# Attention scores in tiles of 64 rows by 32 columns: each block of 32 queries with its own keys only

## The chip, the cores and the metric

The kernel runs on one core of one Trainium2 chip. A core has TensorE (matmuls and the loads of their weights, "PE" and "PEld" in the profile), VectorE ("DVE"), ScalarE ("ACT"), GpSimd ("POOL") and SyncE ("SP", which issues most transfers). The metric is the device time of one execution in microseconds; three runs gave a median of 1027.56 us (1027.11 to 1027.65).

## The reference

The input x holds 64 sequences of 128 tokens with 512 features, in float32. One attention layer is added to it:

```
xn  = layernorm(x, g_in)
q   = (xn @ Wq) as 16 heads of 64, * 64 ** -0.5
k,v = xn @ Wkv, one head of 64 shared by all 16; a null key and a null value are put in front
sim = q @ k + bias            # 16 x 128 x 128 bias, one more for the null key
sim = causal mask, then the mask of the sequence's own tokens
out = softmax(sim) @ v, heads side by side, @ Wo
x   = x + layernorm(out, g_out)
```

A query i sees the null key and keys 0 to i alone. Everything is float32; on TensorE a float32 matmul is carried out in two passes, each a weight load and a matmul.

## The kernel before

**Work and stages.** The 64 sequences are worked in pairs. A *cycle* c handles the softmax of the pair b0, b1, the output product of the pair before (p), the layer norm of the one before that (r), and prepares queries, keys and values for later ones (m). The query projections and the output products are computed as Strassen-like sums: `q_one(c, k, h)` is product k of the query projection for half h, `leaf(c, k, stage)` splits three of them once more, and `out_one(p, k)` is product k of the output. A cycle ends with a *region* (line 1057): the scores of the next pair n0, n1, then the product of probabilities and values of b0, b1. The loop over cycles 1 to 29 calls `cycle` (line 1078); cycle 0 and the end are written out (from line 1294 and from line 1457).

**Order.** The schedule is manual: the order of calls in the source is the order of instructions on every engine, and all that an engine does waits behind what was called before it. TensorE's instructions lie in program blocks of 256; `nc.tensor.addr_align(256, offset=n)` fills up with empty instructions so that the next instruction stands on slot n of a block. It is called once per cycle, ahead of `leaf(c, 3, 0)` (line 1215), and four times in the part before the cycles.

**Layout of the scores.** The 128 queries of a sequence are 4 blocks of 32 (`Q` = 32, `NQ` = 4), the 128 keys likewise. The 16 heads are split over u (2), f (4) and r (2). The 128 rows of a score tile are 4 groups of 32, s = 2 i + u: i tells which query block, u which half of the heads. There are two tiles for a sequence: the lower one (hf = 0) holds query blocks 0 and 1 against the first 64 keys, the upper one (hf = 1) query blocks 3 (i = 0) and 2 (i = 1) against all 128 keys. So no query is multiplied with more than the keys of its tile, though block 0 has 32 keys too many in the lower one and block 2 has 32 too many in the upper one. What is too much is driven to a very negative value by the bias: `bias_add` (POOL, line 631) lays the bias with the causal mask and the mask of the sequence into the score buffer `S[b]` beforehand.

**Scores.** `heads(b, hf, to)` (line 645) makes, for each f, r and i, one matmul with a stationary operand of 64 rows (head features, half r of the partitions) by 64 columns (2 u x 32 queries), and the keys of the tile as the moving operand. That is 16 matmul calls a tile. Four such calls (2 r x 2 i) fill the four quadrants of the array. The results go to banks of PSUM: the upper tile of n0 to `ps_s`, the lower tiles of both to banks a and c of `ps_q`, the upper tile of n1 to the two banks of `ps_w`. `scores_add` (line 682) then adds a tile's banks into `S[b]` on DVE: one addition for the upper tile of n0, two for each other one. `scores_max` and `exps` (ACT) make the softmax from it; `blocks_T` transposes the probabilities on DVE, and `values` multiplies them with the values, in tiles of 32 rows by 64 columns.

**Head of a cycle.** After the region, TensorE goes on with `q_one(c, 1, 0)` (product 1 into bank a), `q_one(c, 5, 0)` (bank c), `leaf(c, 2, 0)` and `q_one(c, 6, 0)` (again bank a). Between products, ACT copies bank a out (`first_into`, line 502). ACT also has to move the values' results out of PSUM (`values_out`, line 794), and DVE the maxima of the scores. From cycle 2 on (`LEAF` = 2) `q_one(c, 7, h)` and `q_one(c, 8, h)` each add bank c into a part of the queries on DVE (lines 1008 and 1016).

Of the kernel before, what the change touches and what calls it, by code (L numbers as in the profile page):

```python
# [8 lines left out]
FP = mybir.dt.float32  # L9
# [8 lines left out]
def kernel(  # L18
# [625 lines left out]

    def heads(b, hf, to):
        g, t = divmod(b, GB)
        for f in range(NF):
            for r in range(2):
                rows = slice(r * DH, (r + 1) * DH)
                for i in range(2):  # L650
                    nc.tensor.matmul(  # L651
                        to[r][i * DH : (i + 1) * DH, f, :],
                        qT[g, f // FH, t // GH][
                            rows, f % FH, t % GH, NQ - 1 - i if hf else i
                        ],
                        kT[g][rows, 0 : NQ if hf else NQ // 2, t, :],
                        start=True,
                        stop=True,
                    )

    def scores_upper(b, pool, tags):
        if len(tags) == 1:
            ps = pool.tile([P, 2, NF, N], FP, tag=tags, name=f"ps_{b}_1")
            heads(b, 1, [ps[:, r] for r in range(2)])
            pss[b, 1] = [(slice(0, R8), ps)]
        else:
            ps = [pool.tile([P, NF, N], FP, tag=t, name=f"ps_{b}_1{r}") for r, t in enumerate(tags)]
            heads(b, 1, ps)
            pss[b, 1] = [(slice(r * NF, (r + 1) * NF), ps[r]) for r in range(2)]

    def scores_lower(bs):
        low = [
            ps_q.tile([P, 2, NF, NL], FP, tag="ac"[r], name=f"ps_{bs[0]}_0{r}")
            for r in range(2)
        ]
        for k, b in enumerate(bs):
            heads(b, 0, [low[r][:, k] for r in range(2)])
            pss[b, 0] = [(slice(r * NF, (r + 1) * NF), low[r][:, k]) for r in range(2)]

    pss = {}  # L680

    def scores_add(b, hf):
        for ks, ps in pss.pop((b, hf)):
            sv = S[b][:, ks, KEYS[hf]]
            if ks.stop - ks.start == R8:
                sv = sv.rearrange("p (r f) j -> p r f j", r=2)
            nc.vector.tensor_tensor(sv, ps, sv, ALU.add)  # L687

# [291 lines left out]
    def q_one(c, k, h):  # L980
# [12 lines left out]
        elif k == 2:  # L993
            product(g, f, 2, ps_w, "w")
            q_out(g, f, lo_t, "w", "p1")
        elif k == 5:
            product(g, f, 5, ps_q, "c")
        elif k == 6:
            product(g, f, 6, ps_q, "a", start=False)
            if c >= LEAF:  # L1000
                first_into(g, f, 1)
            else:
                keep("a", "u2")
        elif k == 7:
            product(g, f, 7, ps_q, "a", start=False)
            if c >= LEAF:
                first_into(g, HC + f, 0)
                nc.vector.tensor_tensor(
                    q_part(g, HC + f, 1), by_block("c"), q_part(g, HC + f, 0), ALU.add
                )  # L1010
            else:
                keep("a", "u3")
                q_out(g, HC + f, hi_t, "c", "u3")
        elif k == 8:
            o = q_part(g, f, 1)
# [62 lines left out]
    def cycle(c):  # L1078
# [21 lines left out]
        if pair:  # L1100
            values_out(p + 1, (0, 2))
        if fin:
# [304 lines left out]
    bias_add(2)  # L1407
    nc.tensor.addr_align(256, offset=40)
    q_one(0, 3, 0)
# [9 lines left out]
    q_one(0, 1, 1)  # L1419
    nc.tensor.addr_align(256, offset=97)  # L1420
    q_one(0, 2, 1)
# [6 lines left out]
    bias_add(3)  # L1428
    nc.tensor.addr_align(256, offset=146)
    q_one(0, 6, 1)  # L1430
# [9 lines left out]
    leaf_weights(4, 2)  # L1440
    nc.tensor.addr_align(256, offset=211)
    q_one(0, 4, 1)
# [198 lines left out]
```

## Time and profile before

| | |
|---|---|
| median of three runs | 1027.56 us |
| span of the profiled execution | 1024.9 us |
| TensorE matmuls busy | 1013.0 us, 12,104 instructions |
| TensorE weight loads busy | 900.7 us, 12,104 instructions |
| VectorE busy | 852.5 us |
| GpSimd busy | 788.2 us |
| ScalarE busy | 642.8 us |
| matmuls of the scores (line 651) | 4,096 instructions, 93.7 us |
| program blocks fetched for TensorE | 96 packets, 1.57 MB |

In a row of groups there stand the source line, the engine, the operation, what is written and read, the shape (for TensorE the tile of the array, rows * columns, then the moving operand), the count, then the busy time, the mean duration of one, and the idle time of the engine before them with what ended it. In a row of the timeline the start and the length of one or more merged instructions come first, both in us. A row of a stretch gives its start and end, its length, then for each engine the busy time and, in brackets, the number of instructions that ran in it, then the granted clock, the DMA share and GB/s. Where a row names no engine order, the order is PE, PEld, DVE, ACT, POOL. A row of the queues gives packets, MB, and the time of the packets as a share of 16 engines over the stretch. Rows of one line's instructions give count, shortest, median and longest duration, and the first and last start; `PEldq` is TensorE's instruction sequencer.

### The profile page before, as it was taken

The numbers are of one execution on the slowest core, as the hardware profiler recorded it, in microseconds if no ns is written. First come the engines' busy times: TensorE is split into PE (matmuls) and PEld (weight loads), VectorE is DVE, ScalarE is ACT, GpSimd is POOL, SyncE is SP. The second block draws the span as 40 slices with busy tenths as digits, with TensorE's granted clock in tenths as the row PEclk, the third lists the DMA queues.
The fourth block names the chain that finished last, engine by engine and source line by source line (L and its number), as shares of the span: only waits on it lengthen the run. The fifth ranks groups of instructions, "written<-read, shape, count | busy, mean of one in ns | idle before, by whom it ended". The sixth has DMA issues, their size and how long they took to land. (4 is left out here: it accounts for less than half of the span.)

```text
span 1024.9 us, 31793 instructions
## 1 busy us (share of the span) xinstructions
PE 1013.0 (99%) x12104; PEld 900.7 (88%) x12104; DVE 852.5 (83%) x2000; ACT 642.8 (63%) x2742; POOL 788.2 (77%) x710
## 2 busy tenths in 40 slices
PE   9999999999999999999999999999999999999997
PEld 8888888888888889888889888889888898888876
DVE  6776887888888888888888878788888888878798
ACT  2655776555776556775556765557765567755591
POOL 3799959688696878959689596887968789596874
PEclk9999999999999999999999999999999999999999
DMA  7542350524315152241623505253151521402203
GB/s 212 165 125 55 104 135 26 158 64 135 107 43 152 49 158 84 93 118 32 171 71 106 135 23 158 64 140 101 46 152 46 157 85 73 111 25 67 84 2 104
DMA packets 70264, 100.91 MB, mean 98 GB/s; under 512 B 27744, under 2 KB 31328, under 8 KB 68320
## 3 DMA queue, kind: packets, MB, share of 16 engines
q1 hardware_dynamic: 69008, 97.83, 33.1%
q8 instruction: 96, 1.57, 0.7%
q10 hardware_dynamic: 1104, 1.05, 0.3%
q14 instruction: 56, 0.46, 0.2%
HBM read 63.19 MB, written 33.55 MB: 94 GB/s over the span
## 5 line engine op out<-in xcount | busy, mean ns | idle before, releaser
L701 ACT ACTIVATE s<-s,nmax 128x65 f32<-128x65 f32 (+1 forms) x1024 | 382.2, 413 | 3.5 <-DVE nmax L692 3.5
L701 ACT ACTIVATION_READ_ACCUMULATOR s<-s,nmax 128x1 f32 x1024 | 242.0, 236 | 0.0
L722 POOL TENSOR_TENSOR s<-s,rinv 128x1024 f32<-128x1024 f32 (+1 forms) x128 | 189.4, 1482 | 46.4 <-DVE rinv L718 46.4
L635 POOL TENSOR_TENSOR s<-biasp,mneg 128x1552 f32<-128x1552 f32 x64 | 205.0, 3224 | 2.0 <-DMA x<-in_x_dram 2.0
L810 ACT ACTIVATE oT<-poX,nv 128x256 f32<-128x256 f32 x58 | 27.5, 474 | 219.2 <-PE poX L770 113.0
L687 DVE TENSOR_TENSOR s<-ps,s 128x256 f32<-128x256 f32 (+2 forms) x224 | 120.0, 605 | 15.7 <-PE ps L651 15.2
L556 DVE TENSOR_TENSOR qT<-pl,qT 128x128 f32<-128x128 f32 (+1 forms) x420 | 122.4, 323 | 3.3 <-PE pl L553 3.3
L860 PE MATMUL pyX<-wo,oT 128*128 128x256 f32 x512 | 121.4, 380 | 0.0
L692 DVE TENSOR_REDUCE nmax<-s 128x8 f32<-128x520 f32 (+1 forms) x128 | 116.5, 949 | 0.1
L860 PE MATMUL pyX<-wT,oT 128*128 128x256 f32 x488 | 115.7, 380 | 0.7 <-POOL oT L843 0.7
L737 DVE STREAM_TRANSPOSE sb<-s 128x1536 f32<-128x1536 f32 x64 | 113.1, 1768 | 0.6 <-POOL s L722 0.6
L860 PEld LDWEIGHTS pyX<-wo,oT 128*128 128x128 f32 x512 | 97.0, 190 | 14.3 <-issue 0.9
L917 POOL TENSOR_TENSOR rstdo<-rstdo,nhalf 128x1 f32<-128x1 f32 x64 | 35.0, 548 | 91.5 <-DVE rstdo L913 91.5
L860 PEld LDWEIGHTS pyX<-wT,oT 128*128 128x128 f32 x488 | 88.4, 191 | 10.8 <-POOL oT L843 1.1
L651 PE MATMUL ps<-kT,qT 64*64 64x128 f32 (+1 forms) x4096 | 93.7, 246 | 0.4 <-issue 0.4
L651 PEld LDWEIGHTS ps<-kT,qT 64*64 64x64 f32 x4096 | 85.5, 134 | 5.5 <-issue 2.1
L770 PE MATMUL pos<-sb,vr 32*64 32x128 f32 (+1 forms) x1792 | 81.4, 321 | 0.0
L843 POOL TENSOR_TENSOR yS<-oT 128x512 f32<-128x512 f32 x32 | 40.8, 1274 | 45.4 <-ACT oT L810 42.0
L770 PE MATMUL poY<-sb,vr 32*64 32x128 f32 x720 | 74.6, 348 | 0.0
L770 PE MATMUL poX<-sb,vr 32*64 32x128 f32 x960 | 73.5, 299 | 0.0
L503 ACT COPY qT<-pa 128x256 f32<-128x256 f32 x168 | 68.2, 406 | 1.4 <-PE pa L597 1.4
L331 DVE STREAM_TRANSPOSE xb<-x 128x512 f32<-128x512 f32 x56 | 39.4, 705 | 34.1 <-ACT x L310 34.1
(150 smaller groups left out, 2545.6 us busy)
## 6 DMA issues: line engine op xcount, KB each, us to landing
res<-in_x_dram SPq DMA_DIRECT2D x64, 256.0 KB, 2.9
out_dram<-y SPq DMA_DIRECT2D x58, 256.0 KB, 2.1
x<-in_x_dram SPq DMA_DIRECT2D x224, 64.0 KB, 2.0
xd<-xb SPq DMA_DIRECT2D x14, 1024.0 KB, 4.3
xT<-xd SPq DMA_DIRECT2D x56, 256.0 KB, 5.4
vr<-vd SPq DMA_DIRECT2D x64, 128.0 KB, 3.3
x<-in_x_dram SPq DMA_DIRECT2D x8, 256.0 KB, 4.8
vd<-vt SPq DMA_DIRECT2D x32, 64.0 KB, 6.2
```

The costliest lines, as they stand in the source:

```text
L503: nc.scalar.copy(q_part(g, c, h), by_block("a"))
L556: nc.vector.tensor_tensor(o, p, o, ALU.add)
L635: nc.gpsimd.tensor_tensor(S[b], biasp, mneg[:, t].unsqueeze(1).broadcast_to([P, R8, ROW]), ALU.add,)
L651: nc.tensor.matmul(to[r][i * DH : (i + 1) * DH, f, :], qT[g, f // FH, t // GH][rows, f % FH, t % GH, NQ - 1 - i if hf else i], kT[g][rows, ...
L687: nc.vector.tensor_tensor(sv, ps, sv, ALU.add)
L692: nc.vector.tensor_reduce(nmax[b][:, hf], S[b][:, :, WITH_NULL[hf]], AX.X, ALU.max, negate=True)
L701: nc.scalar.activation(row, row, AF.Exp, bias=nmax[b][:, hf, k : k + 1], accum_out=rsum[b][:, hf, k : k + 1],)
L722: nc.gpsimd.tensor_tensor(sv, sv, rinvs.pop((b, hf)).unsqueeze(2).broadcast_to([P, R8, sv.shape[2]]), ALU.mult,)
L737: nc.vector.transpose(sb.rearrange("p j e q -> p e j q"), S[b][:, :, 1 : ROW - 1].rearrange("p e (j k) -> p e j k", k=Q),)
L770: nc.tensor.matmul(po[s][rows, half], vr[g][quad(s), j, t, :], sb[quad(s), slots, r * NF : (r + 1) * NF, :], start=start, stop=True, skip_ ...
L843: nc.gpsimd.tensor_tensor(o, l, m, op)
L860: nc.tensor.matmul(prod[key], h[:, c, :], w[:, c, :], start=(start and c == 0), stop=(c == HC - 1), skip_group_check=not start,)
```

## The change

The scores are made of tiles of 64 rows by 32 columns, eight to the array: u is no longer part of the stationary operand's columns, and each block of 32 queries is multiplied with the keys of blocks 0 to its own alone (32, 64, 96 or 128 of them). `region` first reserves the banks of all four tiles and then hands all four to one `heads`, which interleaves them: for each i the columns already streamed are summed up (`at`), and the runs of four calls (2 r x 2 u) are issued in the order of that sum, so that both halves of the array's columns progress alike. In this program each call of `heads` for a region makes 128 matmul calls instead of 64.

`scores_add` makes two additions of each one: all 128 rows for the keys that both query blocks have, and the 64 rows of the later block for the 32 keys beyond.

In the head of a cycle, from cycle 2 on, `q_one(c, 1, 0)` is called one `values_out` earlier (its copy on ACT then stands ahead of the pair's last `values_out` on banks X and Y), the two first `exps` are called behind `q_one(c, 6, 0)`, the addition that belonged to `q_one(c, 7, h)` is made by `q_one(c, 8, h)`, which stands behind `out_one(p, 2)` in the first half and ahead of `leaf(c, 4, 1)` in the second. All alignments move by 27 slots.

```diff
+    def heads(parts):
+        runs = []
+        for i in range(2):
+            at = 0
+            for b, hf, to in parts:
+                block = NQ - 1 - i if hf else i
+                for f in range(NF):
+                    runs.append((at, i, b, block, f, to))
+                    at += block + 1
+        for _, i, b, block, f, to in sorted(runs, key=lambda run: run[:2]):
+            g, t = divmod(b, GB)
+            for r in range(2):
+                rows = slice(r * DH, (r + 1) * DH)
+                for u in range(2):
+                    s = 2 * i + u
+                    nc.tensor.matmul(
+                        to[r][quad(s), f, 0 : (block + 1) * Q],
+                        qT[g, f // FH, t // GH][rows, f % FH, t % GH, block, u],
+                        kT[g][rows, 0 : block + 1, t, :],
+                        start=True,
+                        stop=True,
+                        tile_position=(r * DH, s * Q),
+                    )
...
     def scores_add(b, hf):
+        first = KEYS[hf].start
+        ends = (Q, 2 * Q) if hf == 0 else (3 * Q, 4 * Q)
         for ks, ps in pss.pop((b, hf)):
-            sv = S[b][:, ks, KEYS[hf]]
-            if ks.stop - ks.start == R8:
-                sv = sv.rearrange("p (r f) j -> p r f j", r=2)
-            nc.vector.tensor_tensor(sv, ps, sv, ALU.add)
+            for rows, lo, hi in (
+                (slice(0, P), 0, ends[0]),
+                (slice((1 - hf) * DH, (2 - hf) * DH), ends[0], ends[1]),
+            ):
+                sv = S[b][rows, ks, first + lo : first + hi]
+                if ks.stop - ks.start == R8:
+                    pv = ps[rows, :, :, lo:hi]
+                    sv = sv.rearrange("p (r f) j -> p r f j", r=2)
+                else:
+                    pv = ps[rows, :, lo:hi]
+                nc.vector.tensor_tensor(sv, pv, sv, ALU.add)
...
     def region(c):
-            scores_upper(n0, ps_s, "s")
-            scores_lower((n0, n1))
-            scores_upper(n1, ps_w, "ww")
+            up0 = score_banks(n0, ps_s, "s")
+            low = lower_banks((n0, n1))
+            up1 = score_banks(n1, ps_w, "ww")
+            heads([(n0, 1, up0), (n0, 0, low[0]), (n1, 0, low[1]), (n1, 1, up1)])
...
     def cycle(c):
         if pair:
-            values_out(p + 1, (0, 2))
+            values_out(p + 1, (0,))
+        early = c < LEAF or p < 0
+        if not early:
+            q_one(c, 1, 0)
+        if pair:
+            values_out(p + 1, (2,))
...
-        q_one(c, 1, 0)
+        if early:
+            q_one(c, 1, 0)
...
-        if soft:
-            exps(b0, 0, 0, 2)
         q_one(c, 6, 0)
         if soft:
-            exps(b0, 0, 2, 8)
+            exps(b0, 0)
...
+        out_one(p, 2)
         if c >= LEAF:
             q_one(c, 8, 0)
-        out_one(p, 2)
...
-            nc.tensor.addr_align(256, offset={1: 120, B // 2 - 3: 76}.get(c, 94))
+            nc.tensor.addr_align(256, offset={1: 147, B // 2 - 3: 103}.get(c, 121))
...
         if c >= LEAF:
+            q_one(c, 8, 1)
             leaf(c, 4, 1)
-            q_one(c, 8, 1)
```

`score_banks` and `lower_banks` are the parts of the former `scores_upper` and `scores_lower` that reserve banks; at the end of the kernel these two still exist and call `heads` for one or two tiles.

More of the change, by code (lines that the diff above doesn't have):

```diff
@@ L643, with score_banks, lower_banks @@
     WITH_NULL = slice(0, 1 + NL), slice(1 + NL, ROW)
[L645 to L661, printed above, removed]
+    pss = {}
+    def score_banks(b, pool, tags):
         if len(tags) == 1:
             ps = pool.tile([P, 2, NF, N], FP, tag=tags, name=f"ps_{b}_1")
-            heads(b, 1, [ps[:, r] for r in range(2)])
             pss[b, 1] = [(slice(0, R8), ps)]
[L666 to L671, printed above, removed]
+            return [ps[:, r] for r in range(2)]
+        ps = [pool.tile([P, NF, N], FP, tag=t, name=f"ps_{b}_1{r}") for r, t in enumerate(tags)]
+        pss[b, 1] = [(slice(r * NF, (r + 1) * NF), ps[r]) for r in range(2)]
+        return ps
+    def lower_banks(bs):
         low = [
@@ L676, in scores_lower, with scores_upper @@
         for k, b in enumerate(bs):
[L677 removed]
             pss[b, 0] = [(slice(r * NF, (r + 1) * NF), low[r][:, k]) for r in range(2)]
[L680 removed]
+        return [[low[r][:, k] for r in range(2)] for k in range(len(bs))]
+    def heads(parts):
[21 more added lines that the diff above has]
+                    )
+    def scores_upper(b, pool, tags):
+        heads([(b, 1, score_banks(b, pool, tags))])
+    def scores_lower(bs):
+        low = lower_banks(bs)
+        heads([(b, 0, low[k]) for k, b in enumerate(bs)])
     def scores_add(b, hf):
+        first = KEYS[hf].start
+        ends = (Q, 2 * Q) if hf == 0 else (3 * Q, 4 * Q)
         for ks, ps in pss.pop((b, hf)):
[L684 to L687 removed]
+            for rows, lo, hi in (
[9 more added lines that the diff above has]
+                nc.vector.tensor_tensor(sv, pv, sv, ALU.add)
     def scores_max(b, hf):
```

14 lines of the change are left out of this document (7 added, 7 removed).

## The prediction

> **What bounds the kernel now.** I read the page first, then the groups by form, then stretches of one cycle, and last the instruction queue of TensorE.
>
> ```profile
> span 1024.9 us, 31793 instructions
> PE 1013.0 (99%) x12104; PEld 900.7 (88%) x12104; DVE 852.5 (83%) x2000; ACT 642.8 (63%) x2742; POOL 788.2 (77%) x710
> PEclk9999999999999999999999999999999999999999
> q8 instruction: 96, 1.57, 0.7%
> ```
>
> TensorE has no idle time to give (1013.0 of 1024.9 us), so whatever lengthens its stream lengthens the kernel. The last row is the transfer of its program: 96 packets in 1.57 MB are 16 KB each, and 24,208 matmuls and weight loads over 96 are 252, so a packet is a block of some 256 instructions.
>
> The scores, by form (matmuls, weight loads, the DVE additions that follow), and the two stages of one cycle, scores (499.07 to 501.91) and values (to 504.36):
>
> ```profile
> L651 PEld LDWEIGHTS ps<-kT,qT 64*64 64x64 f32 x4096 | 85.5, 134 | 5.5 <-issue 2.1
> L651 PE MATMUL ps<-kT,qT 64*64 64x128 f32 x2048 | 69.2, 273 | 0.0
> L651 PE MATMUL ps<-kT,qT 64*64 64x64 f32 x2048 | 35.9, 218 | 0.4 <-issue 0.4
> L687 DVE TENSOR_TENSOR s<-ps,s 128x256 f32<-128x256 f32 x128 | 45.2, 413 | 0.0
> L687 DVE TENSOR_TENSOR s<-ps,s 128x1024 f32<-128x1024 f32 x32 | 39.2, 1224 | 15.7 <-PE ps L651 15.2
> ...
> core 0: us, PE busy (x), PEclk, DMA share, GB/s
> 499.07:501.91 2.84, 2.84 (x130) 1.00 0.51 119
> 501.91:504.36 2.45, 2.45 (x116) 1.00 0.88 224
> ```
>
> A region multiplies four score blocks (upper and lower keys of two sequences): 64 calls, each two passes, each a weight load and a matmul: 128 matmuls, 256 instructions in 2.84 us.
>
> **Part 1: the smaller tiles.** *Columns.* A column group streams, per sequence and pass, 4 heads x (128 + 64) = 768 columns today and 4 x (128 + 32) or 4 x (96 + 64) = 640 afterwards, a sixth less. Of the 2.84 us about 0.2 are the change of tile shape, so the stream shrinks from 2.64 to 2.20 us: 0.44 us saved per region, if nothing but the array counts.
>
> *Instructions.* The same work becomes 128 calls, so 512 instructions instead of 256. Can they be supplied? The weight loads of the lower blocks; the stretch before the values (matmuls, then loads); and the marks that the instruction sequencer leaves when it passes into the values (source line 770) and out of them (597):
>
> ```profile
> core 0: us, PEld busy (x), PEclk, DMA share, GB/s
> ...
> 499.98:500.92 0.94, 0.94 (x68) 1.00 0.59 174
> ...
> 501.30:501.91 0.61, 0.61 (x29) 0.44 (x17) 0.61 (x3) 0.00 (x0) 0.00 (x0) 1.00 0.85 121
> ...
> L770 PEldq EVENT_SEMAPHORE  x2: 51/51/51, 501.2 to 501.3; - x2
> ...
> L597 PEldq EVENT_SEMAPHORE  x2: 51/51/51, 503.7 to 504.0; - x2
> ```
>
> In the lower blocks 64 loads and 64 matmuls, 128 instructions, go in 0.93 us: 7.3 ns each, but from a filled queue. Between the marks at 501.3 and 503.7 the sequencer passes the 224 instructions of the values: 10.7 ns each, one block change included. Between these two ends I take 8.3 ns, the value at which weight loads for idle tiles arrive when the queue is dry:
>
> ```profile
> 502.60 0.13 PEld L770 LDWEIGHTS pos<-sb,vr 32*64 32x64 f32 x1
> 502.62 0.13 PEld L770 LDWEIGHTS poX<-sb,vr 32*64 32x64 f32 x1
> 502.62 0.13 PEld L770 LDWEIGHTS pos<-sb,vr 32*64 32x64 f32 x1
> ```
>
> The two loads of pos lie about 17 ns apart, and a load and its matmul are two instructions. At that rate 512 instructions need 4.25 us; the queue holds some 40 at the start (an estimate: when the sequencer marks the values at 501.3, the 29 + 17 score instructions of the second row are still running or to come), which takes off 0.33. So the region would be bound by its instructions at 3.9 us, not by the array at 2.2: 1.3 us more per region (0.8 at 7.3 ns, 2.4 at 10.7).
>
> [...]
>
> *Blocks.* The 256 added instructions are one more program block per region, three where two lie now. The queue's packets around a region, in this order: from 529.8 to 533.7; from 498.8 to 505.5; from 505.5 to 509.4; then one packet in 1.8 us from 498.85, and one in 1.8 us from 809.55:
>
> ```profile
> q8 instruction: 2, 0.03, 4.0%
> ...
> q8 instruction: 1, 0.02, 1.3%
> ...
> q8 instruction: 2, 0.03, 4.2%
> ...
> q8 instruction: 1, 0.02, 4.7%
> ...
> q8 instruction: 1, 0.02, 6.0%
> ```
>
> A packet starts at each end of the first and third windows: 3.8 and 3.8 us apart. Between these, in the cycle that sends the transposed tokens out and back (1 MB each way, DMA share 0.88 in the values), one is 6.7 us after the other. The last two rows are transfers of 16 x 1.8 x 4.7% = 1.35 us and 1.73 us; and only after the long one did the values stop:
>
> ```profile
> 809.70:812.54 2.84, 2.84 (x129) 2.67 (x128) 2.78 (x7) 0.00 (x0) 1.75 (x1) 1.00 0.75 183
> 812.54:815.27 2.73, 2.73 (x116) 2.21 (x112) 2.73 (x6) 0.00 (x0) 0.00 (x0) 1.00 0.89 222
> ...
> 812.73 0.27 PE L770 MATMUL poY<-sb,vr 32*64 32x128 f32 x2
> 812.89 0.32 PE L770 MATMUL pos<-sb,vr 32*64 32x128 f32 x2
> ```
>
> 2.73 us instead of 2.45, with a hole up to 812.89. I read this so: entering a block asks for the next one, which is usable 3.5 us later (the 3.8 us less some room; more under heavy transfers), and there is room for no more than these two. Today blocks change about every 3.7 us here, so it just fits. Afterwards the region starts on a block (the aligned point moves from slot 94 to 121, and 133 instructions of the cycle's code lie between it and the region, which so begins at slot 254 instead of 227): the middle of the region is reached after (258 - 40) x 8.3 = 1.8 us, and only then is the block of the values asked for. It is usable at 1.8 + 3.5 = 5.3 us, and in the cycles with the token transfers 6.7 - 3.8 = 2.9 us later, at 8.2. The values start at 2.84 today. So the price, which contains the 1.3 us above, is 2.5 us in a quiet region and 5.4 in a busy one. Ends: no wait for blocks, 1.3; a busy region with the block still later, 7.
>
> [...]
>
> **Part 2: additions in two.** 7 instructions per region become 14, over the same elements per lane. From 413 ns at 256 and 1224 at 1024 elements, one costs 1.06 ns per element and 0.14 us: 224 x 0.14 = 31 us more on DVE at most, 884 of 1025. They run beside the values and the next products; the longer region covers them. Without that cover: 1 us a cycle. They also must wait for the first upper block, after 36 of 128 calls (16 of 64 today): about the same share.
>
> **Part 3: the head.** What TensorE loses there, by the timeline:
>
> ```profile
> 504.36 1.13 PE L597 MATMUL pa<-xT,wq 128*128 128x256 f32 x4
> 505.33 1.03 PE L597 MATMUL pc<-xS,wS 128*128 128x256 f32 x4
> 506.44 1.13 PE L597 MATMUL pa<-xS,wS 128*128 128x256 f32 x4
> ...
> 506.00 0.39 ACT L503 COPY qT<-pa 128x256 f32<-128x256 f32 x1
> 506.25 1.61 ACT L810 ACTIVATE oT<-pos,nv 128x256 f32<-128x256 f32 x4
> ```
>
> Product 6 waits 0.1 us for ACT's copy of bank a. That copy now goes ahead of one values_out, and the next one ahead of two exponentials, so the 0.1 us goes: 28 x 0.1 = 3 us gained; late next is nothing that the trace shows. TensorE's own order is not changed by these moves. On DVE the additions from bank c come after out_part of product 2 (second half: after tokens_T and out_part, and ahead of leaf 4's two): one addition of 0.41 us in front of two others, and no matmul waits there now; nothing. No DMA and no POOL step moves. The program's alignment by 27 slots costs nothing but the block position above.
>
> **The sum.** 31 regions, 30 with values; the token transfers lie in 14. 16 x 2.5 + 14 x 5.4 = 116; first region 1.3 and the end's three score calls about 1.5; head -3. Together +115 on the profiled execution (span 1024.9; the median of the runs is 2.7 above it, which I leave outside): 1027.6 + 115 = about 1142 us.
>
> **Rivals.** (1) *Supply alone.* Blocks are there in time and only the 8.3 ns count: 31 x 1.3 + 1 - 3 = +38, 1066 us (1049 at 7.3 ns, 1099 at 10.7). For it: the values from 501.91 pass in 2.45 us without such a hole. Against: the hole at 812.89. (2) *The array decides, the change is faster.* If instructions come at under 4.3 ns (2.2 us over 512), each region gains 0.44: 31 x 0.44 + 3 = 17, 1011 us. [...] For it: bursts of loads a few ns apart. Against: the dry stretches and the marks above; from 5.6 ns on ((512 - 40) x 5.6 = 2.64 us) nothing of it is left. (3) *Nothing changes*, gain and supply meet by chance: about 1028.
>
> [...]
>
> **How the numbers follow.** Blocks and supply (forecast) 0.60, its own range 1102 (all regions quiet) to 1170 (busy ones at 7); supply alone 0.26; faster 0.12; no change 0.02. A measurement tells some 0.2% from no change. Leaving out the faster case and the ends of the others gives 1050 to 1178. Faster 0.12, same 0.02, slower 0.86.
>
> **What would show it.** The scores' matmuls 8192, PEld count 16,200. Right: the stage from first score to first value matmul lasts 5.3 us and more, the values still about 2.5 us, with holes in TensorE before the values that are longer where DMA share is high, PE share well under 99%, and q8 at 128 packets. Supply alone would show stages of 4.1 us, all alike. Wrong altogether if that stage lasts under 2.84 us: then the rate of 8.3 ns belonged to the values' own tiles.

## The result, and the profile after

The changed kernel takes 1181.74 us (median of four runs, 1178.7 to 1186.24) against 1027.49 us before: 1.1506 times the time, 95% interval 1.1489 to 1.1523. It is 154 us slower; 115 were forecast, and the range ended at 1178. The profiled execution has a span of 1176.9 us, 152.0 more than before.

From the page of the changed kernel (busy time and instructions of each engine, the granted clock in 40 slices, the queue of TensorE's program, two groups), and behind it, from the page before, the first of these two groups:

```profile
span 1176.9 us, 40240 instructions
PE 1062.2 (90%) x16200; PEld 946.5 (80%) x16200; DVE 891.9 (76%) x2224; ACT 644.3 (55%) x2742; POOL 786.0 (67%) x710
...
PEclk9889989899998999989899898998989999899999
...
q8 instruction: 128, 2.10, 0.7%
...
L795 PE MATMUL poX<-sb,vr 32*64 32x128 f32 x960 | 108.8, 383 | 90.0 <-issue 90.0
...
L681 PEld LDWEIGHTS ps<-kT,qT 64*32 64x32 f32 x8192 | 99.3, 105 | 14.3 <-issue 10.7
```

```profile
L770 PE MATMUL poX<-sb,vr 32*64 32x128 f32 x960 | 73.5, 299 | 0.0
```

TensorE now idles for 10% of the span, and 90 us of that stand ahead of one group: the first bank of the values (line 795, which was 770 and had no idle time). "issue" says that no semaphore the profile shows released it. The packets of the program are 128, as many as predicted. New is the clock row: TensorE no longer has full speed everywhere.

Three stretches of a region, first in a cycle with the transfers of the tokens (14), then in a quiet one, without them (15): the scores up to the first value instruction, the hole, the values behind it (start and end, length, busy time and instructions by engine, granted clock, DMA share, GB/s):

```profile
574.45:577.67 3.22, 3.22 (x257) 3.07 (x256) 3.12 (x9) 0.00 (x0) 1.96 (x1) 1.00 0.69 165
577.67:583.22 5.55, 0.07 (x4) 0.13 (x1) 5.37 (x15) 0.00 (x0) 0.55 (x1) 0.76 0.93 199
583.22:587.28 4.06, 4.06 (x112) 3.85 (x111) 2.25 (x4) 0.00 (x0) 0.00 (x0) 0.50 0.20 58
613.24:616.46 3.22, 3.22 (x257) 3.07 (x256) 2.41 (x8) 0.00 (x0) 3.22 (x3) 1.00 0.03 5
616.46:618.40 1.94, 0.32 (x4) 0.13 (x2) 1.83 (x7) 0.00 (x0) 1.94 (x3) 1.00 0.00 0
618.40:620.66 2.26, 2.26 (x110) 2.18 (x111) 2.19 (x8) 0.00 (x0) 0.57 (x1) 1.00 0.04 7
```

The scores take 3.22 us in both, 0.38 more than before. Then TensorE stands still, 1.94 us in the quiet cycle and 5.55 us where the DMA engines are 93% busy. Behind the long hole the values run at a granted clock of 0.50, called half clock below, and take 4.06 us in place of 2.26. (These stretches end where the last value matmul starts; counted so, the values took 2.15 us before.)

The hole itself, from the timeline of the weight loads (PEld) and of the matmuls (PE):

```profile
577.67 0.13 PEld L795 LDWEIGHTS poX<-sb,vr 32*64 32x64 f32 x1
583.22 0.29 PEld L795 LDWEIGHTS poX<-sb,vr 32*64 32x64 f32 x3 [5.42 <-issue]
...
583.22 0.48 PE L795 MATMUL poX<-sb,vr 32*64 32x128 f32 x2 [5.48 <-issue]
```

One weight load of the values is carried out, and the matmul that belongs to it comes 5.5 us later. The region begins on slot 254; two instructions fill that block, 512 instructions of the scores fill two more but for two slots, and the wait and the first load of the values take these (in cycle 15, where no such wait stands, the first load and its matmul). The hole is exactly where a block ends. It isn't a wait of the values for their operands: that wait was over when the load ran.

The next block arrives ahead of the hole's end. The queue of TensorE's program over 1.4 us, from 580.50 in cycle 14 and from 615.68 in cycle 15:

```profile
q8 instruction: 1, 0.02, 6.0%
...
q8 instruction: 1, 0.02, 5.9%
```

The two packets take 1.35 and 1.31 us. They start 6.07 and 2.46 us into the region, and the values go on 1.35 and 1.39 us after the packet's end. In all of the cycles 0 to 28 the hole ends 1.3 to 1.6 us after the end of such a packet, and the packet takes 0.9 to 1.5 us, with and without the transfers of the tokens. What differs is its start: 2.3 to 3.0 us into the region without them, 4.4 to 6.6 us with them. So the transfers don't stretch the packet, they delay its start; by what way is not shown.

Put together over the cycles (mean differences from before, each taken in the two traces from the first score of one region to that of the next):

| | cycles | first value | values go on | values behind the hole | rest of the cycle | cycle | sum |
|---|---|---|---|---|---|---|---|
| with token transfers (0, 2 to 26) | 14 | +0.38 | +5.43 | +1.79 | +0.14 | +7.36 | 103.1 |
| without (1 to 27, but 5) | 13 | +0.38 | +2.11 | +0.08 | -0.20 | +1.99 | 25.9 |
| 5 and 28 | 2 | +0.38 | +2.44 | +1.41 | +0.10 | +3.95 | 7.9 |
| the first (c = -1) | 1 | | | | | +9.3 | 9.3 |
| 29 and the end | 1 | | | | | +6.2 | 6.2 |

"Values go on" holds "first value" in it. With -0.4 us ahead of the first region the sum is 152.0, the whole difference of the spans.

### The profile page after: what moved, and what is told of

Same layout as the page of the kernel before. It is cut to its first block, busy times and chain, and to the rows that moved or that the text cites. A ratio compares the mean times of both kernels' runs of the same rounds, so it can differ in the third digit from the quotient of the medians.

```text
span 1176.9 us, 40240 instructions
## 1 busy us (share of the span) xinstructions
PE 1062.2 (90%) x16200; PEld 946.5 (80%) x16200; DVE 891.9 (76%) x2224; ACT 644.3 (55%) x2742; POOL 786.0 (67%) x710
## 5 line engine op out<-in xcount | busy, mean ns | idle before, releaser
L726 ACT ACTIVATION_READ_ACCUMULATOR s<-s,nmax 128x1 f32 x1024 | 235.2, 230 | 0.0
L795 PE MATMUL poX<-sb,vr 32*64 32x128 f32 x960 | 108.8, 383 | 90.0 <-issue 90.0
L712 DVE TENSOR_TENSOR s<-ps,s 128x128 f32<-128x128 f32 (+2 forms) x448 | 160.8, 382 | 28.3 <-PE ps L681 23.1
L795 PEld LDWEIGHTS poX<-sb,vr 32*64 32x64 f32 x960 | 86.2, 174 | 96.2 <-issue 91.9
L942 POOL TENSOR_TENSOR rstdo<-rstdo,nhalf 128x1 f32<-128x1 f32 x64 | 35.1, 549 | 128.5 <-DVE rstdo L938 128.4
L681 PE MATMUL ps<-kT,qT 64*32 64x32 f32 (+3 forms) x8192 | 107.5, 238 | 8.5 <-issue 8.5
L681 PEld LDWEIGHTS ps<-kT,qT 64*32 64x32 f32 x8192 | 99.3, 105 | 14.3 <-issue 10.7
L795 PE MATMUL pos<-sb,vr 32*64 32x128 f32 (+1 forms) x1792 | 109.6, 404 | 0.0
L795 PE MATMUL poY<-sb,vr 32*64 32x128 f32 x720 | 103.0, 447 | 2.7 <-issue 2.7
L743 DVE RECIPROCAL rinv<-rsum 128x8 f32<-128x8 f32 x128 | 23.7, 186 | 91.8 <-ACT s L726 91.7
```

The source lines that it names most:

```text
L681: nc.tensor.matmul(to[r][quad(s), f, 0 : (block + 1) * Q], qT[g, f // FH, t // GH][rows, f % FH, t % GH, block, u], kT[g][rows, 0 : block ...
L712: nc.vector.tensor_tensor(sv, pv, sv, ALU.add)
L726: nc.scalar.activation(row, row, AF.Exp, bias=nmax[b][:, hf, k : k + 1], accum_out=rsum[b][:, hf, k : k + 1],)
L795: nc.tensor.matmul(po[s][rows, half], vr[g][quad(s), j, t, :], sb[quad(s), slots, r * NF : (r + 1) * NF, :], start=start, stop=True, skip_ ...
L942: nc.gpsimd.tensor_tensor(yn[b][1], yn[b][1], nhalf, ALU.pow)
```

## The experiments

The forecast's theory is that a program block of 256 instructions is usable some 3.5 us after the block ahead of it was entered (its estimate, from packets 3.8 us apart), later under transfers. Its rivals: the values wait for something that the change makes late; small tiles or many instructions cost by themselves. Each run is compared with the kernel before on the same chip; the ratio's 95% interval is in brackets.

**Own keys without small tiles.** The new scores, additions and head, but tiles of 64 rows by 64 columns, so 256 instructions a region; once with all alignments 10 slots later (region on slot 8), once as in the kernel after (slot 254).

```diff
-                for u in range(2):
-                    s = 2 * i + u
-                    nc.tensor.matmul(to[r][quad(s), f, 0 : (block + 1) * Q],
-                        qT[...][rows, f % FH, t % GH, block, u], kT[g][rows, 0 : block + 1, t, :],
-                        ..., tile_position=(r * DH, s * Q))
+                nc.tensor.matmul(to[r][i * DH : (i + 1) * DH, f, 0 : (block + 1) * Q],
+                    qT[...][rows, f % FH, t % GH, block], kT[g][rows, 0 : block + 1, t, :], ...)
...
-    nc.tensor.addr_align(256, offset={1: 147, B // 2 - 3: 103}.get(c, 121))
+    nc.tensor.addr_align(256, offset={1: 157, B // 2 - 3: 113}.get(c, 131))   # slot 8 alone
```

> The kernel after with tiles of 64 rows by 64 columns (so 256 instead of 512 instructions in a region) that are multiplied with their own keys only, and all alignments 10 slots later, so that a region begins on slot 8 of a program block. Theory of the program blocks (a block is usable some 3.5 us after the one ahead of it was entered): the block ends lie 248 instructions into the region and 24 instructions behind its end; the block after next is asked for at about 1.8 us and usable at 5.2 to 5.3, when TensorE is not yet through with the 24 instructions of the head. So no hole: the first score to the first value matmul takes 2.4 us, the values 2.15, granted clock 1.00 throughout, 0.44 us less per region and 3 to 5 us for the head: 1009 to 1013 us. Rival (the values wait for a semaphore that the new order or the split additions make late): holes of 1.6 us and more stay ahead of the values, 1080 us and over. Rival (weight loads for 64 columns do not fit in 32 streamed columns): scores stay at 2.8 us, about 1023 us.

> As the run with slot 8, but with the alignments of the kernel after, so that the region begins on slot 254 and the values on a block. Theory of the program blocks: the second block of the region is entered some 0.4 us ahead of the region, the third is usable some 3.1 us into it, the values would begin at 2.4: a hole of 0.5 to 0.8 us at the first value matmul in quiet regions, longer by up to 3 us in regions with the token transfers: 1015 to 1050 us, at least 5 us slower than with slot 8. Rivals that do not know of blocks: the same time as with slot 8 within 2 us.

Measured: 1070.34 us on slot 8 (1.0418 [1.0402, 1.0433]) and 1051.47 us on slot 254 (1.024 [1.0223, 1.0257]). With 256 instructions there is no hole between scores and values at all, so what the values wait for in the kernel after is neither the new order nor the additions. Nearly everything else in these two expectations failed. The stages of a quiet cycle on slot 254 (scores, values), then from its timeline a matmul of product 1 of the second half:

```profile
415.80:418.63 2.83, 2.83 (x129) 2.65 (x128) 2.09 (x7) 0.00 (x0) 2.83 (x2) 1.00 0.00 0
418.63:420.78 2.15, 2.15 (x115) 2.04 (x112) 2.02 (x8) 0.00 (x0) 2.15 (x3) 1.00 0.03 8
```

```profile
428.88 0.70 PE L597 MATMUL pa<-xT,wq 128*128 128x256 f32 x2 [0.40 <-ACT qT L503]
```

The scores take 2.83 us with 640 columns streamed per column group, sequences and passes as in the prediction, where they took 2.84 with 768. So in tiles of 64 columns the number of streamed columns did not set the time of the scores, and the 0.44 us were not to be had. The last rival of the first expectation, that the loads of 64 weight columns take this long, named 2.8 us and agrees; no run tests it by itself. And the quiet cycles are 31.55 us, 0.46 longer than before, from a wait for ACT's copy of bank a. On slot 254 no hole is seen in quiet cycles, where 0.5 to 0.8 us were expected: the second block's packet starts 2.28 us ahead of the region, not 0.4. By an estimate TensorE's instruction sequencer is then at least some 25 instructions ahead: in the trace of the kernel after, 23 to 25 matmuls and weight loads start in the 2.28 us ahead of a region (cycles 9, 11, 14 and 15). In its cycles with transfers the next block, which begins 514 instructions behind the region's start, is late in the output product of the next head (by 1.66 us in cycle 12); from cycle 2 on they take 31.6 to 32.6 us. On slot 8 the block behind the values comes late in the cycles with transfers, in the products of the next head (timeline, cycle 12):

```profile
463.78 0.27 PE L553 MATMUL pl<-xT,wq 128*128 128x128 f32 x1
465.77 0.27 PE L553 MATMUL pl<-xT,wq 128*128 128x128 f32 x1 [1.71 <-issue]
```

Its packet started at 462.78 us. These cycles take 32.2 to 35.3 us. So the theory of blocks also says why slot 8 is the worse one, but that was seen afterwards.

**Additions alone.** The kernel before with `scores_add` of the kernel after.

> The kernel before with the additions in two alone (scores, head and alignments as before). Theory, after the run with 64-column tiles, where every quiet cycle had one wait of 0.66 us at the first product of the second half: the seven more additions (7 x 0.14 us) push DVE's maxima and with them ACT's exponentials and its copy of bank a behind the point at which TensorE wants it, and only the longer regions of the kernel after cover this. Then 0.4 to 0.7 us in 29 cycles: 1040 to 1048 us. Rival, as the prediction has it (hidden beside other work): 1027.5 us.

Measured: 1055.01 us (1.0273 [1.0257, 1.0289]). From its timeline:

```profile
424.70 0.81 PE L870 MATMUL pyX<-wo,oT 128*128 128x256 f32 x3
426.07 1.13 PE L597 MATMUL pa<-xS,wq 128*128 128x256 f32 x4 [0.56 <-ACT qT L503]
```

A cycle takes 32.01 us in place of 31.09: TensorE waits for ACT's copy of bank a. On ACT that copy stands behind exponentials, and these wait for DVE's maxima, which stand behind the additions (that this is the way the delay takes is read from the order of the calls). More than expected: 28 us. In the kernel after the rest of a quiet cycle is 0.20 us shorter than before, so there the longer region does hide all of it.

**Head alone.** The kernel before with the cycle's head (and product 8's addition) of the kernel after.

> The kernel before with the new head of the cycle alone (scores, additions and alignments as before). In the trace after the change, the part of a quiet cycle from the last value matmul to the next region lasts 25.91 us against 26.10 before. Theory (the head frees TensorE of a wait on ACT's copy of bank a): 0.1 to 0.2 us in 28 cycles, 3 to 5 us faster, 1022.5 to 1024.5 us. Rival (the shorter rest comes from work that the longer region hides): no difference, 1027.5 us. If the head costs something, over 1028 us.

Measured: 1031.0 us (1.0031 [1.0013, 1.0048]), ten runs from 1024.54 to 1033.4. A quiet cycle is 30.90 us against 31.09, as expected; but some of the cycles with transfers lose more than all that. Cycle 26 (scores, hole, what is left of the values):

```profile
873.32:876.16 2.84, 2.84 (x130) 2.67 (x129) 2.78 (x7) 0.00 (x0) 1.95 (x1) 1.00 0.88 220
876.16:879.03 2.87, 0.46 (x18) 0.23 (x15) 2.84 (x7) 0.00 (x0) 0.00 (x0) 1.00 1.05 212
879.03:882.11 3.08, 3.08 (x99) 2.87 (x98) 3.04 (x7) 0.00 (x0) 0.55 (x1) 0.64 0.56 123
```

A block comes late with 256 instructions too, and the clock falls (0.64 over the third stretch). Here the packet started 2.86 us into the region; before, 0.14 us ahead of it.

**The block end moved.** The kernel after with 128 added to the offset of every alignment (249 in place of 121 in most cycles), so that the region begins on slot 126.

> The kernel after, all alignments 128 slots later: the region begins on slot 126. Theory of the program blocks: there are two holes in a quiet region, one behind instruction 386 of the scores (from 2.3 to about 4.0 us) and one in the middle of the values, behind instruction 642 (about 1.4 us), and none between the scores and the values; a quiet cycle takes 34 to 34.8 us in place of 33.1, one with transfers 39 to 42; 1205 to 1260 us. Rival (the hole belongs to the values, by a semaphore or a buffer): it stays at their first instruction, and the time stays within 1165 to 1195 us.

Measured: 1208.69 us (1.177 [1.1749, 1.1792]). One quiet cycle (9): scores, hole, scores up to the values and their first half, hole, second half:

```profile
418.66:420.85 2.19, 2.19 (x194) 2.19 (x193) 1.41 (x5) 0.00 (x0) 2.19 (x2) 1.00 0.03 7
420.85:422.69 1.84, 0.25 (x22) 0.06 (x9) 0.36 (x2) 0.00 (x0) 1.84 (x2) 1.00 0.00 0
422.69:424.95 2.26, 2.26 (x127) 2.05 (x128) 1.86 (x7) 0.00 (x0) 1.63 (x2) 1.00 0.03 7
424.95:426.25 1.30, 0.24 (x11) 0.00 (x0) 1.26 (x5) 0.00 (x0) 0.00 (x0) 1.00 0.00 0
426.25:427.19 0.94, 0.94 (x47) 0.85 (x47) 0.94 (x3) 0.00 (x0) 0.00 (x0) 1.00 0.00 0
```

The hole has left the first value instruction and stands inside the scores, behind 194 + 193 instructions (386 were predicted), at 2.2 us; a second one is in the middle of the values. The work and its waits are the same: the holes move with the block ends. The quiet cycles take 34.2 to 35.1 us, the time lies at the lower end of what was expected. Not all of the loss against the changed kernel is in the regions: 12 of the 30 us between the profiled executions lie in the first cycle (51.10 us in place of 39.15), where the alignments put in 128 more empty instructions.

**The reads of the tokens moved.** The kernel after with the four reads (1 MB) behind the next cycle's fetch of the values in SP's queue.

```diff
         if first and toks:
             tokens_out(m // GB)
...
-        if first and toks:
-            tokens_in(m // GB)
...
             values_fetch(fetch)
+        if not first and LEAF < c and m - 2 < B:
+            tokens_in((m - 2) // GB)
```

> The kernel after, with the reads of the transposed tokens (1 MB in four transfers) moved in SP's queue from ahead of a region to behind the next cycle's fetch of the values, so that they run after the region. Theory (the transfers hold up the program block by 2 to 4 us, and the longer hole also lets the granted clock fall to half): the regions with token transfers become like the others, hole of 1.5 to 2.2 us in place of 3.9 to 5.9, values 2.26 us in place of 4.06, cycles of 33 us in place of 38: 13 x 5 = 65 to 75 us faster than the kernel after, 1105 to 1120 us. Rival (the holes of these regions have another cause, such as work of the even cycles on DVE or POOL): no change, 1180 us.

Measured: 1131.22 us (1.1024 [1.0998, 1.105]): 50 us less than the changed kernel, not 65 to 75. Cycle 14 (first value, hole, values):

```profile
552.89:556.42 3.53, 3.41 (x257) 3.15 (x256) 3.13 (x9) 0.00 (x0) 1.94 (x1) 1.00 0.22 36
556.42:558.68 2.26, 0.08 (x3) 0.13 (x1) 2.15 (x7) 0.00 (x0) 0.00 (x0) 1.00 0.36 75
558.68:562.41 3.73, 3.73 (x111) 3.53 (x111) 3.66 (x10) 0.00 (x0) 0.55 (x1) 0.57 0.58 159
```

The hole is 2.26 us in place of 5.55. But the scores are 0.3 us longer (a block is late inside them too), and the clock still fell in eight of these cycles.

**The writes left out as well.** The same, and from the fourth group on no write of the transposed tokens.

```diff
     def tokens_out(g):
+        if g > 2:
+            xbs.pop(g)
+            xds[g] = xds[2]
+            return
```

> The kernel after with the reads of the tokens moved behind the next cycle's fetch, and without the writes of the transposed tokens from the fourth group on (the reads take the third group's again; these tokens' values are left out of the result). No large transfer is then under way while a region's blocks are fetched, from cycle 2 on. Theory: what is left in the cycles with transfers in the run with the moved reads (34 to 35.5 us, a hole of 0.3 to 1.1 us inside the scores, half clock in half of them) comes from the writes: all cycles become like the others, 32.9 to 33.5 us, holes of 1.5 to 2.1 us, hardly a window of half clock: 13 x 1.8 = 23 us less than 1131, 1103 to 1113 us. If these cycles are slower for another reason: 1125 to 1132 us.

Measured: 1117.57 us (1.0887 [1.0865, 1.091]), between the two expectations and nearer to the theory's. Cycles 14 and 16:

```profile
543.58:546.81 3.23, 3.23 (x257) 3.08 (x256) 3.13 (x9) 0.00 (x0) 1.94 (x1) 1.00 0.15 26
546.81:548.82 2.01, 0.07 (x3) 0.13 (x1) 1.90 (x7) 0.00 (x0) 0.00 (x0) 1.00 0.54 109
548.82:551.08 2.26, 2.26 (x111) 2.18 (x111) 2.19 (x8) 0.00 (x0) 0.00 (x0) 1.00 0.43 142
...
613.24:615.22 1.98, 0.07 (x3) 0.13 (x1) 1.86 (x7) 0.00 (x0) 0.00 (x0) 1.00 0.42 77
615.22:619.06 3.84, 3.83 (x110) 3.76 (x111) 3.77 (x9) 0.00 (x0) 0.55 (x1) 0.56 0.48 136
```

Ten of the 13 cycles from 2 on now take 32.9 to 33.7 us, like the others. The other three (10, 16, 18) take 35.0 to 35.4, with a window of half clock; two of them have holes no longer than cycle 14's. What the transfers cost is thereby shown: beyond the 1.99 us that a cycle without them loses, the 14 cycles lost 75 us in the changed kernel (103.1 less 14 x 1.99), 28 with the reads moved, and 12 here (their cycles sum to 56.2 and 40.3 us more than before). Of these 12, 4 are cycle 0, whose transfers are still there, and 6 the three windows of half clock.

**Half of the tiles small.** The kernel after with 64x64 tiles for the upper blocks: 384 instructions a region.

```diff
+                if hf:
+                    nc.tensor.matmul(to[r][i * DH : (i + 1) * DH, f, 0 : (block + 1) * Q],
+                        qT[...][rows, f % FH, t % GH, block], kT[g][rows, 0 : block + 1, t, :], ...)
+                    continue
                 for u in range(2):
```

> The kernel after with tiles of 64x32 for the two lower blocks only and of 64x64 for the two upper ones (own keys in both): 384 instructions in a region in place of 512 or 256. If a pair of load and matmul takes 20.6 ns in 64x64 and 11.9 ns in 64x32 tiles (2.64 us over 128 pairs, 3.05 over 256), the scores take 64 x 20.6 + 128 x 11.9 = 2.85 us. Theory of the program blocks: the block end that stood behind the scores now stands 130 instructions into the values, TensorE is there at 4.3 us and the block is usable at 4.9 to 5.1: a hole of 0.5 to 1 us in the middle of the values in quiet regions (1.6 us at 512 instructions, none at 256), longer by 2 to 4 us in the others; quiet cycles 31.6 to 32.2 us, 1065 to 1100 us. Rival (small tiles or many instructions cost by themselves, in proportion): quiet cycles half way between 31.55 (256) and 33.05 (512), with the loss in the scores and no hole.

Measured: 1392.79 us (1.3565 [1.3535, 1.3596]). The time says nothing on the question, for a reason that I had not seen: 384 is no multiple of 256, so the alignment has to fill up each cycle with some 130 empty instructions where 4 to 8 stood. These keep TensorE from 490.2 to 500.1 us of one cycle (134 of them), 74 ns each. The regions can still be read. The stretch with the empty instructions, cycle 9 (scores to first value, values) and the hole in the values of cycle 8, by stretches; then the empty instructions as the trace lists their line (1254), at 13 ns each:

```profile
490.20:500.10 9.90, 3.63 (x19) 2.91 (x17) 3.38 (x11) 7.90 (x37) 7.94 (x9) 0.89 0.17 55
472.65:476.44 3.79, 3.79 (x193) 3.20 (x192) 2.45 (x8) 0.00 (x0) 3.79 (x3) 1.00 0.02 4
476.44:478.85 2.41, 2.41 (x115) 2.13 (x112) 2.29 (x8) 0.00 (x0) 1.59 (x2) 1.00 0.00 0
...
433.02:435.38 2.36, 0.27 (x15) 0.03 (x2) 2.32 (x7) 0.00 (x0) 0.00 (x0) 1.00 0.37 89
```

```profile
L1254 PEldq NOP  x3892: 13/13/13, 106.4 to 1312.2; - x195
```

The scores take 3.79 us to the first value, not 2.85 + 0.2: the change between tile shapes inside them isn't free (two starts 0.2 us apart are seen in each region), and my price per pair missed the rest. The quiet cycle 9 has no hole, where 0.5 to 1 us were expected; the one with transfers has one of 2.36 us, in the middle of the values, where the block end is now. Both fit the theory of blocks, since the scores take 0.7 us longer than I reckoned and the block is usable by then; but that was read off afterwards.

**A version that keeps what is good.** The head alone, with alignments 8 slots later (region on slot 235); then also with the reads of the tokens moved as above; then with them moved only behind the sending of the values and keys; and this last move without the head.

```diff
         if first and toks:
             tokens_out(m // GB)
...
-        if first and toks:
-            tokens_in(m // GB)
...
             keys_send(send)
+        if first and toks:
+            tokens_in(m // GB)
         region(c)
```

> The new head of the cycle alone, as in the run of it, but all alignments 8 slots later (region on slot 235 in place of 227), so that TensorE enters the region's second block some 0.4 us earlier. Theory (with the new head alone the block of the values is asked for some 0.3 us later than before, and comes too late in some of the cycles with token transfers, which is what made that run unsteady): the late blocks go, and the 0.13 to 0.19 us a cycle are left: 1022 to 1025 us in all runs. Rival (the unsteady part is something else): 1024 to 1034 us as before, scattered.

> The same, and the reads of the transposed tokens moved behind the next cycle's fetch of the values. Theory: no block is late any more; 1022 to 1023.5 us, no cycle with a hole ahead of or in the values. If the moved reads make the keys and values of the next cycle late, a new wait ahead of the key-value product, over 1028 us.

> The new head with the region on slot 235, and the reads of the transposed tokens moved only behind the sending of the values and keys (2 to 3 us later than before, 3 us earlier than in the run that moved them behind the fetch). Theory: the block of the values comes before the reads begin, and the reads still end before the key-value product of the next cycle: no hole in the values, no wait of 1.4 us ahead of that product; 1022 to 1024 us, the first run faster than the kernel before. If the stalls of cycles 2, 24 and 26 do not come from the reads: 1027 to 1031 us as without this move.

> The kernel before with the reads of the transposed tokens moved behind the sending of the values and keys, and nothing else. Theory: only the three late blocks of the kernel before (0.23 to 0.27 us each) can go, so 1026 to 1027.3 us, no difference that counts; the 4 us of the run with the new head then belong to the head and the 0.13 to 0.19 us a cycle. If the move itself is the gain: 1023 to 1024.5 us.

Measured: 1028.84 us (1.0022 [1.0012, 1.0032]) for the slots alone, with late blocks in cycles 2, 6, 8 and 26, so 8 slots were not enough; 1037.94 (1.0107 [1.0094, 1.0121]) with the reads moved far, where the next key-value product waits for the tokens that it reads. The row puts the wait down to DVE, but the last of the four reads lands at 457.00:

```profile
457.20 1.10 PE L358 MATMUL pkv<-xT,wkv 128*128 128x256 f32 x4 [1.35 <-DVE qT L556]
```

With the short move 1023.39 us (0.9965 [0.9951, 0.9978]), the only version faster than the kernel before, by 0.35%; the move without the head makes no difference, 1026.87 (0.9998 [0.9989, 1.0007]). Cycle 26 of the fast version (scores, values) and a whole cycle:

```profile
868.73:871.57 2.84, 2.84 (x129) 2.67 (x128) 2.78 (x7) 0.00 (x0) 1.94 (x1) 1.00 0.11 21
871.57:873.77 2.20, 2.20 (x115) 2.12 (x112) 2.20 (x6) 0.00 (x0) 0.00 (x0) 1.00 0.68 144
...
405.06:435.96 30.90, 30.90 (x379) 27.72 (x378) 25.65 (x63) 20.18 (x86) 29.26 (x31) 1.00 0.26 87
```

The DMA share during the scores is 0.11 where it was 0.88 with the head alone, and the hole is gone. So the head of the change is worth 3.5 us (1026.87 less 1023.39), once the block of the values is not made late by it.

## Why the prediction was wrong, and where it was right

The direction and the mechanism, late blocks, were right; the time lies above the range. The step that failed is that of the values behind the stops: the sum holds them at their old length ("the values still about 2.5 us") and has no term for a lower clock, and the half clock there cost 28 us. The second is the first region, taken at 1.3 us and measured at 9.3. Of the 37 us that the forecast was short on the profiled execution these two are 36; the rest are smaller terms of both signs.

**Blocks: right, and nearly in its numbers.** Forecast: the values start at 5.3 us in a quiet region and 8.2 in a busy one, +2.5 and +5.4. Measured +2.11 and +5.43. That the second pair agrees so closely is luck in part: with instructions at 6.0 ns in place of 8.3 the block would have been asked for 0.5 us earlier, and the transfers delayed it by 3.3 us on the mean (2.2 to 4.2 by cycle), not 2.9. The move of the alignments by 128 slots shows that the block ends set the place of the holes, the runs with moved and left-out transfers that the transfers lengthen them. A small point was off: the hole stands behind the first load of the values, not ahead of the values.

**Half clock: the term that was missing, and the cause of the miss.** The prediction forecast stops of several us in 14 regions and yet has no term for the clock in its sum; the values, said to last "still about 2.5 us", took 4.06 in cycle 14. The half clock cost 14 x 1.79 = 25 us in the values of the busy cycles (behind the holes of the other 13 cycles, where full clock stayed, they are 0.08 longer) and 2 x 1.4 in cycles 5 and 28. With the 25 us the sum would have been 1167 us. The half-clock stretches of the changed kernel's trace last 3.41 us (three) and 6.83 us (14), but for the one in which the span ends, and all begin on one grid of 3.41 us. An idle window was not needed: those below ahead of a half-clock window have 0.60, 0.75 and 1.75 us of matmul time.

The windows, around the hole of cycle 14, then one ahead of and one behind the hole's end in cycle 5 and in cycle 11:

```profile
577.14:580.56 3.42, 0.60 (x43) 0.51 (x28) 3.28 (x11) 0.00 (x0) 0.00 (x0) 1.00 1.06 218
580.56:583.97 3.41, 0.75 (x26) 0.75 (x33) 3.34 (x8) 0.00 (x0) 0.55 (x1) 0.50 0.62 141
583.97:587.38 3.41, 3.41 (x102) 3.10 (x86) 1.50 (x3) 0.00 (x0) 0.00 (x0) 0.50 0.26 81
587.38:590.79 3.41, 3.41 (x30) 2.82 (x17) 0.83 (x3) 2.91 (x9) 0.00 (x0) 1.00 0.30 84
...
256.29:259.70 3.41, 1.75 (x111) 1.41 (x99) 3.27 (x11) 0.00 (x0) 3.41 (x3) 1.00 0.02 5
259.70:263.11 3.41, 3.41 (x97) 3.41 (x103) 3.34 (x9) 0.00 (x0) 1.42 (x4) 0.50 0.02 5
471.33:474.74 3.41, 2.31 (x172) 1.96 (x167) 3.29 (x9) 0.00 (x0) 3.41 (x4) 1.00 0.02 5
474.74:478.16 3.42, 2.83 (x112) 2.45 (x113) 3.31 (x11) 0.07 (x1) 1.59 (x3) 1.00 0.02 5
```

In cycle 14 the window with 0.60 us of matmul time is followed by one at half clock, that one, with 0.75 us, by another, and this, busy for all of its 3.41 us, by full clock. Cycles 5 and 11 have holes of 1.98 and 2.01 us. In cycle 5 the hole fell into one window (1.75 us busy) and the next ran at 0.50; in cycle 11 it fell over two (2.31 and 2.83) and the clock stayed at 1.00: 34.92 against 33.40 us for the whole cycle. No run took the clock away by itself; this pair is what isolates it.

**The range: its upper end was no sum.** A busy region at 7 us gives 16 x 2.5 + 14 x 7 with the other terms, 1165 us; 1170 was written, and for 1178 as the end of the range no working is shown.

**Supply of instructions: wrong in size.** Forecast 8.3 ns each and first values at 3.9 us or later by that alone; measured 512 instructions in 3.05 us, 6.0 ns, and the first value at 3.22 (+0.38 for +1.3). The dry stretch of the values from which 8.3 was taken has tiles of 32 by 64. It did little harm, as the wait for the block contained it. Rival 1, supply alone, would by this have given about 31 x 0.4, or 12 us. Over the whole stage a matmul comes every 11.9 ns (3.05 us over 256).

**Columns: wrong.** The stream was to shrink from 2.64 to 2.20 us; with 64x64 tiles it stayed at 2.83 to the first value. Rival 2 rested on this and had no ground: in tiles of 64 columns there was nothing to gain from fewer streamed columns. What does set 2.64 us is open; 256 instructions are not it either, as 512 pass in 3.05.

**Additions: right in the changed kernel.** They are hidden there; and the price given for the case without cover, 1 us a cycle, was measured at 0.92 when they were made alone. Their cost on DVE itself was not "31 us more on DVE at most": the group went from 120.0 to 160.8 us, 40.8 more.

**Head: right in sign and nearly in size** (0.20 us in quiet cycles, where 0.1 was taken; 3.5 us in the run that keeps it, where 3 were), but "late next is nothing that the trace shows" was wrong for the head on its own: the packet of the next block starts later in the region (in quiet cycles at 0.1 to 0.5 us, before at -0.2 to 0.0), and that was late next.

**First region and the end: too small.** Taken at 1.3 and 1.5 us; measured +9.3, and +6.2 for cycle 29 (2.5 of it forecast as a quiet region) and the end. In the first region a block is 4.65 us late, under the start's transfers, with 6.83 us of half clock behind it:

```profile
35.70:40.40 4.70, 0.05 (x5) 0.04 (x7) 0.16 (x1) 0.00 (x0) 4.20 (x4) 0.73 0.64 208
37.84:44.67 6.83, 4.31 (x73) 3.58 (x74) 3.67 (x9) 1.44 (x8) 2.06 (x2) 0.50 0.44 125
```

The prediction had priced this region at the supply of instructions alone, without blocks; but it has the same 512 instructions. Some 6.3 of the 9.3 us are this stop and the half clock. The other 3.0 come later in the cycle, at an alignment with 57 empty instructions where 30 stood. So the alignment by 27 slots did not cost "nothing but the block position above": on slot 254 with 64x64 tiles, where no block is late in the first region, the same 27 empty instructions go with a first cycle of 31.79 us in place of 29.84.

## What to carry to other kernels

Count instructions against the program's blocks wherever a stage issues them as fast as here, at 6.0 ns each: two blocks' worth in 3.05 us weren't refilled in time (2.1 us lost), and with transfers in the same stretch it was 5.4 us. It showed as idle time "issue" on TensorE at a fixed place (90.0 us on line 795), even between a load and its matmul. Where a forecast makes a stop in TensorE, price the half clock behind it as well, and price it for each region that has the stop (here 1.79 us on the mean in the 14 cycles with transfers, 1.4 in cycles 5 and 28, 0.08 in the other 13). And when a change bundles parts, look for the good one: here the head, with the transfers kept away from the block fetch, is 4 us faster than before, while the small tiles cost 130 us against tiles of 64 columns on the same slot (1181.74 less 1051.47).

## What was not expected of the hardware

- The clock fell behind a window of 3.41 us that was half busy (1.75 us, cycle 5), not only behind an idle one (0.00 us from 293.84); so a hole of 2.0 us went with a cycle of 34.92 us in cycle 5 and of 33.40 in cycle 11, by where it fell on the grid. Over the changed kernel's trace, windows at full clock with under 0.40 of matmul time were all followed by half clock, and none with over 0.52 was; of three between, those at 0.45 and 0.50 were not and the one at 0.51 (cycle 5) was (worked out from the matmul records on the grid of the clock's changes). So no sharp limit is seen.
- The empty instructions of an alignment were not free where there were many: 134 took 9.9 us, 74 ns each.
- Fewer streamed columns did not shorten the scores: 2.83 us with 640 per column group, 2.84 with 768, both in 64x64 tiles.
